# Attention and a depthwise convolution on one core: statistics of x closer together, conv weights prepared in image 2, matrices counted by the planner

## The chip, the core and the metric

The kernel runs on one core of a Trainium2 chip. A core has five engines that work side by side, each through its own list of instructions in order: TensorE (PE in the profile), VectorE (DVE), ScalarE (ACT), GpSimd (POOL) and SyncE (SP), which here only issues transfers. ACT and POOL issue transfers too. An instruction that waits on its engine holds up all that is queued behind it. The metric is the device time of one execution in microseconds (us).

## The reference

The input x has 16 images of 384 channels and 32 x 32 pixels, float32. Two layers with a residual follow each other:

```python
x = x + attention(gn(x))        # 8 heads of 48, 1024 tokens, q k v and a projection with bias
x = x + dwconv(gn(x), w_sym)    # 7 x 7 depthwise, padding 3
# gn(v): (v - mean) / sqrt(var + 1e-5) over each of 32 groups of 12 channels
# w_sym: mean of the weight and its three rotations by 90 degrees
```

In the text, "x" is the input and "x1" is the result of the first layer.

## The kernel before

The channels lie on the partitions, in three tiles of 128 per image. For each of the 16 images, PE makes q and k (`qk_step`, L417) and v (`v_step`, L443), then for 4 pairs of heads the scores (`s_step`, L468), whose exponential ACT takes (L476), and their product with v (`av_step`, L484), which also gives the sums for the softmax. These sums go through DRAM to a layout in which DVE inverts them (`invert`, L509) and back as a broadcast tile, with which DVE multiplies (`divide`, L520). Projection (`proj_step`, L537) and a transfer that adds x (L552) make x1. Its statistics come from ACT (`x1_means`, `x1_squares`), go through DRAM on POOL's queue to a layout by group, through DVE (`x1_aggregate`, L277) and ACT (`groups_x1`, L283 to 285) to a scale and a shift, and back through DRAM on POOL's queue (`spread`: gr_x at L254, sc_x at L258). ACT then normalises x1 (xn, L334). The depthwise convolution is 49 taps per channel tile on DVE (`conv_tap`, L602), each one a multiply and add of a shifted picture; three chains of taps, one per channel tile, run in turn. While PE does image b + 1, DVE does the taps of image b.

The last two images share the convolution with PE. There, for two of three channel tiles (one is split), matmuls with small diagonal matrices do it (`conv_on_pe`, L708). The matrices are made on DVE by `conv_matrices` (L666, four products each, two calls in the last image) from `wsh` and `eye`, which `conv_prepare` makes on POOL: a memset of `zero`, two transfers to DRAM, sixteen small ones back to `wsh`, eight that write zero borders in DRAM, and four small instructions for `eye`. In the kernel before it is called in image 1, after the first eight steps (L1214).

The scale of the input x is needed ahead of each image. Image 0 does its own at the start, image 1 by `x_channels` and `x_groups`, which use the Newton steps of `inverse_sigma` on DVE (L207 to L222). All the others are done in one stream during image 0: `stream_in` loads the 42 tiles (L350), `stream_stats` takes BN statistics (L357), `stream_gather` and `stream_groups` turn them by way of DRAM into `x_sc`. `stream_groups` ends with a power on POOL (L392).

The order of the instructions is written by a planner in the kernel's Python, which keeps two clocks: `clock` for PE and `vclock` for DVE. `after(wait, cost, f)` puts work in a heap with a due time and what it will take of DVE; `catch_up` lets DVE's list run up to PE's clock: due work first, otherwise the next tap, at the price of `us_tap`. A due time decides only a place in the lists, and every engine then runs its list as its waits allow. The prices that matter here are the 0.045 us that `us_tap` adds per tap in the last image (`late_us`) and the work of `conv_matrices`, which has no price.

At the end of the last image there is a different path (`divide_at_once`, L563 to L566, `proj_part`, L574, `residual`, L583): DVE inverts the sums directly (L565), PE projects, DVE adds and takes statistics, PE averages them by group (`groups_on_pe`, L302), and the taps and matmuls of what is left of images 14 and 15 follow, until `conv_on_pe_end` (L723) and the last output.

Of the kernel before, what the change touches and what calls it, by code (L numbers as in the profile page):

```python
# [44 lines left out]
def kernel(  # L45
# [64 lines left out]
    def run(general):  # L110
        tag = "g" if general else "f"
        with ExitStack() as stack:
# [233 lines left out]
            def stream_in(b, k):  # L346
                if not many:
                    many["bs"] = npool.tile([P, B - 2, NK, 12], F32, tag="xn1", name="bs_all")
                many[b, k] = rpool.tile([P, N], F32, tag="x1", name=f"xs_{b}_{k}")
                nc.gpsimd.dma_start(  # L350
                    many[b, k], x[b, k * P : (k + 1) * P].rearrange("p h w -> p (h w)")
                )

            def stream_stats(b, k):
                t = many.pop((b, k))
                for h in range(2):
                    nc.vector.bn_stats(  # L357
                        many["bs"][:, b - 2, k, 6 * h : 6 * h + 6], t[:, h * HALF : (h + 1) * HALF]
                    )
# [22 lines left out]
            def stream_groups():  # L382
                M = B - 2
                mv = small.tile([P, 4, 2], F32, tag="mva", name="mv_all")
                nc.vector.memset(mv, 1.0)
                for q in range(4):
                    n = min(P, M * GROUPS - q * P)
                    nc.vector.bn_aggr(mv[0:n, q], many["gs"][0:n, q])
                af = small.tile([P, 4, 2], F32, tag="afa", name="af_all")
                ve = small.tile([P, 4], F32, tag="vea", name="ve_all")  # L390
                nc.vector.tensor_scalar(ve, mv[:, :, 1], EPS, None, ALU.add)
                nc.gpsimd.tensor_tensor(af[:, :, 0], ve, mhalf, ALU.pow)  # L392
                nc.vector.scalar_tensor_tensor(
                    af[:, :, 1], mv[:, :, 0], -1.0, af[:, :, 0], ALU.mult, ALU.mult
                )
                gr_d = ddram.tile([M * GROUPS, PER, 2], F32, tag="gra", name="gr_all")
                with nc.allow_non_contiguous_dma(reason="once"):
                    for q in range(4):
                        n = min(P, M * GROUPS - q * P)
                        nc.gpsimd.dma_start(  # L400
                            gr_d[q * P : q * P + n],
                            af[0:n, q].unsqueeze(1).to_broadcast([n, PER, 2]),
                        )
                    rows = gr_d.rearrange("(b g) e s -> b (g e) s", b=M)
                    for k in range(NK):
                        nc.gpsimd.dma_start(
                            x_sc[:, 2:, k, :], rows[:, k * P : (k + 1) * P].rearrange("b p s -> p b s")
                        )
# [252 lines left out]

            def conv_matrices(n, dst):

                dst = dst[:, 0 : SH * 2 * KS * CH].rearrange("p (i t c) -> p i t c", i=SH, c=CH)
                for i in range(SH):
                    nc.vector.tensor_tensor(  # L666
                        dst[:, i],
                        eye.unsqueeze(1).to_broadcast([P, 2 * KS, CH]),
                        wsh[:, n, i].rearrange("p b d -> p (b d)").unsqueeze(2).to_broadcast(
                            [P, 2 * KS, CH]  # L670
                        ),
                        ALU.mult,
                    )
                mats[PE_K[n]] = dst

            def conv_store(b, k):
                nc.sync.dma_start(xds[b, k][:, PAD * W : (PAD + H) * W], xn1s[b, k])
# [138 lines left out]
            def after(wait, cost, f):  # L816

                nonlocal count
                count += 1
                heapq.heappush(later, (now() + wait, count, cost, f))  # L820

            def us_tap(dy, dx):
                late_us = 0.045 if clock > last_image else 0.0
                rows = H - abs(dy)
                if tuple(active[0][0:2]) == SHARED:
                    rows = min(H - max(0, dy), SPLIT) - max(0, -dy)
                return (rows * (W - abs(dx)) + (128 if len(active) > 1 else 268)) / 955 + late_us
# [239 lines left out]
            issue(chunks.popleft())  # L1067
            every = [(b, k) for b in range(2, B) for k in range(NK)]
            for n, bk in enumerate(every):
                after(3.0 * n, 0.0, lambda bk=bk: stream_in(*bk))  # L1070
                after(3.0 * n + 10.0, 1.4, lambda bk=bk: stream_stats(*bk))
            after(3.0 * len(every) + 14.0, 0.0, stream_gather)
            after(3.0 * len(every) + 34.0, 3.6, stream_groups)

            EARLY = NP * (B - 4)

# [92 lines left out]
            for b, n0, size in [  # L1169
                (b, b * PER_B + sum(SIZES[:g]), SIZES[g]) for b in range(B) for g in range(len(SIZES))  # L1170
            ]:
                r = n0 - b * PER_B
                if n0 == NS - PER_B:
                    last_image = clock
                if r % (2 * NT) == 0 and r // (2 * NT) < NK:
                    while chunks and chunks[0][1:] <= (b, r // (2 * NT)):
                        issue(chunks.popleft())
                for n in range(n0, n0 + size):
                    s_step(n)
                clock += (size * US_STEP + US_TURN) / 2  # L1180
                if r == 0:
                    for i in range(NT // 2):
                        issue(("v", b, i))
                ending = b == B - 1 and r + size == PER_B
                if ending:
                    catch_up(clock)
                    divide_at_once(NP * b + NP - 1, 0)
                    vclock += 4.2
                    for o in range(NK):
                        proj_part(b, o, (0, 1))  # L1190
                    loads(1)
                    clock += 2 * US_PROJ
                else:
                    catch_up(clock)
                    act_slot(4.5)
                    other(n0 + size, False)
                for n in range(n0, n0 + size):
                    av_step(n)
                    u, h, i = n // (2 * NT), n // NT % 2, n % NT
                    if i == NT - 1:  # L1200
                        take(u, h)
                clock += (size * US_STEP + US_TURN) / 2
                if n0 // (2 * NT) < (n0 + size) // (2 * NT):
                    finish((n0 + size) // (2 * NT) - 1)
                if ending:
                    catch_up(clock)
                    assert not invs and not waiting
                    fast_finish(b)
                else:
                    other(n0 + size, True)  # L1210
                if b == B - 4 and r == 32:
                    after(0.0, 2.0, check_early)
                if b == 1 and r == 0:
                    conv_prepare()  # L1214
                if b == B - 1:

                    if once("mat_0", r >= 16):
                        mat = flat2(xpool.tile([P, NK, N], F32, tag="x", name="mat_0"))
                        conv_matrices(0, mat)
                        late["w3"] = mat[:, 2 * SH * KS * CH :][:, 0:C]  # L1220
                    if once("w", r >= 32 and b - 1 in x1_stats):
                        nc.sync.dma_start(wp, w4[:, 0:NK])
                        nc.sync.dma_start(late["w3"], w4[:, NK])
                    if once("mat_1", r >= 24):
                        conv_matrices(1, flat2(qkpool.tile([P, 2, N], F32, tag="qk", name="mat_1")))
                    if once("ones", r >= 32):
                        t = opool.tile([P, N], F32, tag="o", name="masks_1")
                        nc.sync.dma_start(t, masks.rearrange("p b c -> p (b c)"))
                        late["masks"] = t.rearrange("p (b c) -> p b c", c=P)
                if b == B - 1:  # L1230
                    if r >= 32 and (b, 0) not in x1s and all(c[0] > b - 2 for c in active):
                        for k in range(NK):
                            x1s[b, k] = rpool.tile([P, N], F32, tag="x1", name=f"x1_{b}_{k}")
                            nc.gpsimd.dma_start(
                                x1s[b, k], x[b, k * P : (k + 1) * P].rearrange("p h w -> p (h w)")
                            )
                if b == B - 1 and r in (32, 40, 48):
                    loads(1)
# [63 lines left out]
```

## Time and profile before

| | |
|---|---|
| median of 4 runs | 2942.09 us (2939.54 to 2944.22) |
| the profiled execution | 2943.35 us |
| its span, first to last instruction | 2941.3 us |
| PE busy | 2903.3 us, 99% |
| DVE busy | 2573.6 us, 88% |
| ACT busy | 1442.6 us, 49% |
| POOL busy | 192.6 us, 7% |
| mean granted clock of PE | 0.994 |

The profile gives times in us from the start of the span. A line of a timeline has the start, the duration, the engine, the line of the kernel, the operation, what it writes and reads, and how many instructions were merged; in brackets stands how long the engine was idle before it, and what ended the wait. A line of waits has who waited, for whom, the total, how often, and the longest. A line of stretches has the stretch and its length, then busy time and count for PE, PE's weight loads, DVE, ACT and POOL, then PE's granted clock, the share of the DMA engines and GB/s.

### The profile page before, as it was taken

How to read it: one execution, taken by the hardware profiler on the slowest of the kernel's cores; microseconds unless marked ns; L12 is line 12 of the kernel's file. 1: busy time of each engine (PE TensorE's matmuls, PEld its weight loads, DVE VectorE, ACT ScalarE, POOL GpSimd, SP SyncE). 2: the span in 40 equal slices, each digit the busy share in tenths (PEclk: the TensorE clock that was granted, in tenths of full speed). 3: DMA queues.
4: the chain of work that ended last, by engine and by line, in shares of the span. 5: the costliest groups of instructions: out<-in, count | busy, mean ns of one | idle time of the engine just before them, and what ended most of it. 6: DMA issues, size and time to landing. Idle time of an engine off the chain costs nothing.

```text
span 2941.3 us, 30279 instructions
## 1 busy us (share of the span) xinstructions
PE 2903.3 (99%) x11554; PEld 1175.6 (40%) x11554; DVE 2573.6 (88%) x2546; ACT 1442.6 (49%) x1724; POOL 192.6 (7%) x305
## 2 busy tenths in 40 slices
PE   8999999999999999999999999999999999999987
PEld 4343343433434343343434434343343434334333
DVE  4322998989999898999989899898999989899898
ACT  2545545464454555445464554546545365554610
POOL 2113000000100001000000100000010000100000
PEclk9999999999999999999999999999999999999999
DMA  6423012120302203022220301213021221301424
GB/s 233 143 63 70 16 35 69 37 68 16 83 22 42 69 21 84 16 40 64 42 63 24 84 20 35 69 29 76 16 64 41 42 63 27 83 16 35 117 61 116
DMA packets 72539, 169.84 MB, mean 58 GB/s; under 512 B 30416, under 2 KB 32352, under 8 KB 70848
## 3 DMA queue, kind: packets, MB, share of 16 engines
q0 software_dynamic: 29456, 96.08, 12.9%
q1 hardware_dynamic: 41328, 68.44, 9.8%
q10 hardware_dynamic: 1600, 3.28, 0.5%
q8 instruction: 93, 1.52, 0.2%
q14 instruction: 62, 0.51, 0.1%
HBM read 119.92 MB, written 29.36 MB: 51 GB/s over the span
## 4 chain that ended last, share of the span: by engine, by line


## 5 line engine op out<-in xcount | busy, mean ns | idle before, releaser
L602 DVE SCALAR_TENSOR_TENSOR x<-xn,wsym,x 128x899 f32<-128x899 f32 (+11 forms) x2181 | 2372.2, 1169 | 109.2 <-ACT xn L334 109.2
L476 ACT ACTIVATE e<-ps_s 128x1024 f32<-128x1024 f32 x1024 | 952.5, 1054 | 55.7 <-PE ps_s L468 52.8
L468 PE MATMUL ps_s<-qk 48*128 48x512 f32 x4096 | 916.3, 597 | 3.0 <-ACT qk L424 3.0
L484 PE MATMUL acc<-e,v 128*64 128x512 f32 x4096 | 907.2, 595 | 0.0
L468 PEld LDWEIGHTS ps_s<-qk 48*128 48x128 f32 x4096 | 377.4, 186 | 538.1 <-ACT e L476 256.9
L484 PEld LDWEIGHTS acc<-e,v 128*64 128x64 f32 x4096 | 283.1, 137 | 608.1 <-issue 599.0
L417 PE MATMUL ps_qk<-x,wqk 128*128 128x512 f32 x1152 | 508.7, 598 | 2.4 <-DVE x L330 2.4
L495 ACT COPY o<-acc 128x512 f32<-128x512 f32 x128 | 75.1, 587 | 603.9 <-PE acc L484 603.8
L417 PEld LDWEIGHTS ps_qk<-x,wqk 128*128 128x128 f32 x1152 | 217.5, 191 | 289.9 <-issue 287.4
L443 PE MATMUL ps_v<-wv,x 128*128 128x384 f32 x768 | 252.0, 488 | 0.0
L537 PE MATMUL ps_proj<-o,wp 128*128 128x512 f32 x540 | 234.6, 593 | 1.0 <-DMA o<-o 1.0
L424 ACT COPY qk<-ps_qk 128x1024 f32<-128x1024 f32 x96 | 96.5, 1006 | 241.7 <-PE ps_qk L417 241.6
L443 PEld LDWEIGHTS ps_v<-wv,x 128*128 128x128 f32 x768 | 144.8, 190 | 109.5 <-ACT e L476 12.1
L520 DVE TENSOR_TENSOR o<-o,inv 128x1024 f32<-128x1024 f32 x63 | 77.3, 1227 | 99.9 <-DMA inv<-inv 80.2
L552 POOL DMA_DIRECT2D x<-in_x x45 | 39.2, 870 | 1869.3 <-ACT x L545 1736.3
L537 PEld LDWEIGHTS ps_proj<-o,wp 128*128 128x128 f32 x540 | 102.3, 190 | 128.3 <-issue 124.2
L452 ACT COPY v<-ps_v 128x384 f32<-128x384 f32 x128 | 55.1, 483 | 185.6 <-PE ps_v L443 185.6
L545 ACT ACTIVATE x<-ps_proj,bp 128x1024 f32<-128x1024 f32 x45 | 50.1, 1113 | 184.7 <-PE ps_proj L537 184.7
L334 ACT ACTIVATE xn<-x,sc_x 128x1024 f32<-128x1024 f32 x46 | 53.8, 1231 | 101.6 <-DMA sc_x<-gr_x 68.5
L509 DVE RECIPROCAL rec<-sums 128x16 f32<-128x16 f32 x63 | 16.0, 254 | 78.5 <-DMA sums<-sum 78.5
L708 PE MATMUL ps_conv<-sh,mat 128*32 128x464 f32 (+7 forms) x784 | 72.9, 527 | 1.6 <-DMA sh<-xd 1.6
L357 DVE BATCH_NORM_STATS2 bs_all<-xs 128x6 f32<-128x512 f32 x84 | 51.9, 680 | 12.1 <-DMA xs<-in_x 12.1
(113 smaller groups left out, 505.8 us busy)
## 6 DMA issues: line engine op xcount, KB each, us to landing
x<-in_x POOLq DMA_DIRECT2D x90, 512.0 KB, 5.6
inv<-inv SPq DMA_DIRECT2D x126, 256.0 KB
out<-x POOLq DMA_DIRECT2D x48, 512.0 KB, 7.5
xs<-in_x POOLq DMA_DIRECT2D x42, 512.0 KB, 6.1
qk<-qk SPq DMA_DIRECT2D x96, 128.0 KB
o<-o SPq DMA_DIRECT2D x90, 64.0 KB
sh<-xd SPq DMA_DIRECT2D x36, 160.0 KB
sh<-xd ACTq DMA_DIRECT2D x20, 160.0 KB
```

The lines of the kernel that those rows point to most:

```text
L417: nc.tensor.matmul(ps[:, h, :], lhsT=wqk[:, k, s, t, :], rhs=xns[b][:, k, h * HALF : (h + 1) * HALF], start=(k == 0), stop=(k == NK - 1),)
L424: nc.scalar.copy(halves(qks[u][:, s, :]), ps)
L443: nc.tensor.matmul(ps[:, j, 0:C], lhsT=xns[b][:, k, t * P : (t + 1) * P], rhs=wv[:, k, :], start=(k == 0), stop=(k == NK - 1),)
L452: nc.scalar.copy(dst.rearrange("p (h d) -> p h d", d=D + 1)[:, :, 0:D], ps[:, j, 0:C].rearrange("p (h d) -> p h d", d=D),)
L468: nc.tensor.matmul(ps[:, j, :], lhsT=qks[u][r, 1, i * P : (i + 1) * P], rhs=qks[u][r, 0, h * HALF : (h + 1) * HALF], start=True, stop=True,)
L476: nc.scalar.activation(es[n], ps, AF.Exp, scale=SCALE)
L484: nc.tensor.matmul(accs[u, h][64 * j : 64 * j + 64, :], lhsT=v_of(u, i, j), rhs=e[:, j, :], start=(i == 0), stop=(i == NT - 1),)
L495: nc.scalar.copy(os_[u][:, h * HALF : (h + 1) * HALF], accs.pop((u, h)))
L520: nc.vector.tensor_tensor(os_[u], os_[u], invs.pop(u), ALU.mult)
L537: nc.tensor.matmul(ps[:, h, :], lhsT=wp[:, t, o * P : (o + 1) * P], rhs=os_[NP * b + t][:, h * HALF : (h + 1) * HALF], start=(t == 0), sto ...
L602: nc.vector.scalar_tensor_tensor(acc, xn1s[b, k].rearrange("p (h w) -> p h w", w=W)[:, iy, ix], wsym[:, k, dy + PAD, dx + PAD : dx + PAD + 1],
L708: nc.tensor.matmul(pss[b, k][CH * i : CH * (i + 1), h, :].rearrange("p (y x) -> p y x", x=W)[:, y0:, ox], lhsT=mats[k][:, i, d0 * KS + dx ...
```

## The change

Five edits. `stream_groups` calls `inverse_sigma` on DVE for all groups in place of a power on POOL between two DVE instructions. The stream's tiles are planned 2.0 us apart instead of 3.0, with the gather and the groups moved accordingly, and their costs to the planner are 0.6 and 6.0 instead of 0.0 and 3.6. `conv_prepare` is called in image 2 after the step group that starts at 40, instead of image 1 after the first. `conv_matrices` advances `vclock` by 2.2 per call. `late_us` is 0.02 instead of 0.045.

```diff
                 af = small.tile([P, 4, 2], F32, tag="afa", name="af_all")
-                ve = small.tile([P, 4], F32, tag="vea", name="ve_all")
-                nc.vector.tensor_scalar(ve, mv[:, :, 1], EPS, None, ALU.add)
-                nc.gpsimd.tensor_tensor(af[:, :, 0], ve, mhalf, ALU.pow)
-                nc.vector.scalar_tensor_tensor(
-                    af[:, :, 1], mv[:, :, 0], -1.0, af[:, :, 0], ALU.mult, ALU.mult
-                )
+                inverse_sigma(af, mv[:, :, 0], mv[:, :, 1], "all")
...
             def conv_matrices(n, dst):
+                nonlocal vclock
...
                 mats[PE_K[n]] = dst
+                vclock += 2.2
...
-                late_us = 0.045 if clock > last_image else 0.0
+                late_us = 0.02 if clock > last_image else 0.0
...
-                after(3.0 * n, 0.0, lambda bk=bk: stream_in(*bk))
-                after(3.0 * n + 10.0, 1.4, lambda bk=bk: stream_stats(*bk))
-            after(3.0 * len(every) + 14.0, 0.0, stream_gather)
-            after(3.0 * len(every) + 34.0, 3.6, stream_groups)
+                after(2.0 * n, 0.0, lambda bk=bk: stream_in(*bk))
+                after(2.0 * n + 10.0, 1.4, lambda bk=bk: stream_stats(*bk))
+            after(2.0 * len(every) + 14.0, 0.6, stream_gather)
+            after(2.0 * len(every) + 34.0, 6.0, stream_groups)
...
-                if b == 1 and r == 0:
+                if b == 2 and r == 40:
                     conv_prepare()
```

## The prediction

> **What bounds the kernel.** I read the page first (the chain that ended last is empty there), then PE's waits, then the timelines around every PE gap, and the stretches at the end.
>
> ```profile
> PE 2903.3 (99%) x11554; PEld 1175.6 (40%) x11554; DVE 2573.6 (88%) x2546; ACT 1442.6 (49%) x1724; POOL 192.6 (7%) x305
> ```
>
> PE is idle for 38.0 of 2941.3 us: 8.1 before 20 us, 18.2 after it ends at about 2923, the rest in few places. The waits of PE name them:
>
> ```profile
> PE ps_proj L574 <- DVE o L566: 5.8, 1, 5.8
> ...
> PE ps_s L468 <- ACT qk L424: 3.0, 2, 1.9
> ...
> PE ps_conv L708 <- DMA sh<-xd: 1.6, 1, 1.6
> ```
>
> So only what removes a PE gap, or shortens the head or the tail, can pay. The 1.9 us is in image 1. The timelines of POOL, ACT and PE there:
>
> ```profile
> 259.24 0.29 ACT L285 ACTIVATE af_x<-mv_x,af_x 32x1 f32<-32x1 f32 x1
> ...
> 260.51 0.90 POOL L660 TENSOR_TENSOR eye<-eye,ident 128x32 f32<-128x32 f32 x3
> ...
> 261.71 0.64 POOL L254 DMA_DIRECT2D gr_x<-af_x  x1 [0.30 <-issue]
> ...
> 270.65 3.50 ACT L334 ACTIVATE xn<-x,sc_x 128x1024 f32<-128x1024 f32 x3 [8.39 <-DMA sc_x<-gr_x]
> ...
> 272.06 1.13 PE L468 MATMUL ps_s<-qk 48*128 48x512 f32 x4
> ...
> 275.10 7.97 PE L468 MATMUL ps_s<-qk 48*128 48x512 f32 x28 [1.91 <-ACT qk L424]
> ...
> 283.00 7.09 PE L484 MATMUL acc<-e,v 128*64 128x512 f32 x32
> ```
>
> The scale of image 0's x1 was ready at 259.53, but POOL was still in `conv_prepare` (244.29 to 261.4) and issued it at 261.71. ACT then waited 8.39 us, the qk evictions (L424) stood behind it, and PE stopped. The same place one image later, with no `conv_prepare` ahead:
>
> ```profile
> 445.83 3.50 ACT L334 ACTIVATE xn<-x,sc_x 128x1024 f32<-128x1024 f32 x3 [4.59 <-DMA sc_x<-gr_x]
> ...
> 451.04 7.14 PE L468 MATMUL ps_s<-qk 48*128 48x512 f32 x32
> 458.11 7.09 PE L484 MATMUL acc<-e,v 128*64 128x512 f32 x32
> ```
>
> From the first L468 to L484 it takes 7.07 us here, and 10.94 in image 1: 3.87 us are lost there. The stretches show why that is more than the wait of 1.91, and the same in the tail (the first figures are PE's busy time, the 0.50 is the granted clock):
>
> ```profile
> 276.00:278.00 2.00, 2.00 (x8) 0.99 (x8) 2.00 (x4) 1.79 (x2) 0.00 (x0) 0.50 0.97 383
> ...
> 2836.00:2839.00 3.00, 0.38 (x1) 0.38 (x2) 2.91 (x3) 0.00 (x0) 0.00 (x0) 0.50 0.00 0
> 2839.00:2841.00 2.00, 2.00 (x3) 0.79 (x3) 1.84 (x3) 0.00 (x0) 0.00 (x0) 0.50 0.00 0
> ```
>
> In the tail DVE is the bound: from 2747.66 it runs without a gap to 2840.6, and its last instruction closes the kernel, 5 us after PE's last matmul:
>
> ```profile
> 2834.43 3.36 DVE L565 RECIPROCAL inv<-ps_sum 128x512 f32<-128x512 f32 x1
> ...
> 2838.62 6.57 PE L574 MATMUL ps_proj<-o,mat 128*128 128x512 f32 x10 [5.78 <-DVE o L566]
> ...
> 2927.75 1.22 DVE L723 TENSOR_TENSOR x<-ps_conv,x 128x1024 f32<-128x1024 f32 x1
> ```
>
> **What the Trainium skill says.** "TensorE: Matmul & The Clock Gate", Part 1: PE's clock is halved after an idle window of about 3.4 us and restored after a busy one, and the windows run freely, so where they fall differs from run to run. The trace agrees, with less idle than that: half clock from 275.9 to 279.3, after a gap of 1.9 us, and from 2835.9 to 2842.7, stretches of 3.4 and 6.8 us. "DMA: Bandwidth & Descriptors", Anatomy of one DMA: a DMA from GpSimd costs about 2 us fixed. The hop gr_x to sc_x here takes 4.3 us from issue to issue, and wsh 1.9 to landing. The same page, Issuing engines are not separate DMA queues: all share 16 engines; it fits sum to sums taking 3.5 us beside `conv_prepare` (262.29 to 265.77) against 2.2 one image later.
>
> **The change, part by part.** In the instruction orders of the changed program PE, ACT and SP are unchanged; only DVE and POOL differ.
>
> *conv_prepare in image 2.* 17.1 us of POOL work leave the place ahead of gr_x. gr_x is then issued 0.3 us after 259.53, at 259.8; by the row at 445.83 xn begins 5.29 us after the qk matmuls (440.54), so at 261.56 + 5.29 = 266.9 instead of 270.65. Three applies take 3.5, to 270.4; the first qk is ready at 266.9 and the second at 272.1, as in image 2. PE does not stop: gain 3.87 us in this profile, made of 2.16 waiting and half of 3.41 = 1.71 at half clock. Even if sc_x comes only 1.9 us earlier (what POOL gives back), xn starts at 268.8 and about 3.4 of it remains. But the clock part needs the idle 1.91 to fall well inside one window, (3.41-1.91)/3.41 = 44% of positions, so in a median I count half of 1.71: 2.16 + 0.85 = 3.0. From there to image 14 all is paced by PE, and DVE waits for xn every image (109 us in 15 waits), so the shift is kept.
> At its new place it stands behind the loads of x for image 3 (issued by 453.0), and POOL has nothing else until 575.55, a wait of 122.56 us. Its first memset needs a tile whose last reader is a divide; even with the one at 504.98 it is done by 523. The x1 adds (L552) are behind it, 52 us later; the inverse that reuses its tile is loaded at 559. Cost 0; with the cover gone, up to 17.1 us.
>
> *x statistics at 2.0 instead of 3.0.* 42 loads and 84 BN statistics of 0.68 us come earlier. DVE did them in image 0 in gaps (it idles 46.5 us at the first reciprocal), so they cost nothing. What moves is image 1's own scale: x_channels and x_groups now stand behind more of them, and the reciprocal of pair 1 behind these. bs_x follows the divide at 111.43 and one more statistic: it ends at 117.5 (116.2 before). gs_x is then issued at 120.2; nine statistics lie ahead of the aggregate, five loaded, four whose loads are issued behind gs_x and land from about 126 to 130 (6.1 us each, 1.25 apart). Aggregate 131, 2.3 for the Newton steps, gr_x 134, sc_x issued at 138.3 and landed at 140.8. ACT takes it at 147.69 after eight exponentials, so 7 us are spare, and 2.2 more ahead of the next copy. Cost 0; bounds 0 to what exceeds 149.7. The group aggregates then end near 158, when the third reciprocal (158.47) gets its sums; projection needs the last divide at 209.84.
>
> *Newton instead of the power on POOL.* 12 more DVE instructions at 0.18 us pitch = 2.2 us, less a POOL hop of 1.3 (172.93 to 174.26). DVE idles 29 us right behind, and image 2 needs x_sc at 284. Cost 0.
>
> *The last image's order.* Matrices are now counted (2 x 2.2 us) and taps 0.025 us cheaper. As built: both reciprocals and divides of the last pairs come two or three taps earlier, and L565/L566 twice: two taps (812 and 841 elements, 2.1 us) that stood ahead now stand behind. L566 ends at 2836.5 instead of 2838.56, so PE's gap falls from 5.78 to 3.7 us. But DVE gets the same instructions: what follows begins 2.1 us earlier and has 2.1 us more to do. As many taps stand ahead of the wait at L1101 as before. So the end moves by nothing, except for DVE's own waits on PE (2.72 at L316, 0.3 at L583): PE at half clock for 2.8 instead of 4.1 us saves up to 0.65 there. I take 0.4, between 0 and 2.9. The sums of pairs 61 and 62 were requested at 2760.3 and 2790.7, more than 10 us ahead of their moved reciprocals: no new wait.
>
> **Sum.** Against the profiled execution: 2941.3 - 3.87 - 0.4 = 2937.0, plus 2.05 around the span = 2939.1. That execution (2943.35) lies 1.26 above the median of the runs, which a clock window that not all runs pay would explain. On the median: 2942.09 - 3.0 - 0.4 = 2938.7.
>
> **Rivals.**
> 1. *The tail passes its gain on.* For: PE's gap shrinks by 2.1 and DVE waits 7.4 us for PE and POOL after 2840. Against: those waits move as a whole. It would be 2942.09 - 3.0 - 2.9 = 2936.2.
> 2. *The transfer is late anyway.* For: sc_x took 4.6 us from issue to apply at 266, beside six qk copies on SP; if these, and not POOL, hold it, the change does not do what it says. Against: 2.4 us at 2721.79. Gain 0.2: 2941.9.
> 3. *Slower: image 1's scale late in image 0.* Behind more statistics and loads, sc_x misses 149.7, the last moment at which three applies of 3.56 meet the qk matmuls at 153.29. Each microsecond more is paid in full, and 1.7 for the clock. It eats the gain of 3.4 from a landing at about 151.4; at 160 the kernel is at 2942.1 - 3.4 + 10.3 + 1.7 = 2950.7. Against: 9 us between 140.8 and 149.7.
>
> **How the numbers follow.** This kernel's runs tell a difference from about 0.2% (5.9 us). Forecast 0.66 (own range 2936.5 to 2940.5), rival 1 0.15, rival 2 0.10, rival 3 0.09. Faster by over 0.2% means below 2936.2: half of rival 1 (0.075) and a seventh of the forecast, for where the clock windows fall (0.095), 0.17. Slower, above 2948: rival 3, 0.09. Same: the rest, 0.74. The range for 8 in 10 reaches from rival 1's lower half to just over no gain: 2935.0 to 2943.0.
>
> **What would show it.** Right: no PE wait on ACT qk in image 1, gr_x issued near 259.8, and L468 to L484 in 7.1 us; ACT's apply near 147.7 without a wait; `conv_prepare` in POOL's hole of image 2; PE's gap at L574 near 3.7 us; DVE still last. Wrong: a new wait at L334 in image 0, xn still near 270, or a PE gap in image 2 or 3.

## The result, and the profile after

| | before | after |
|---|---|---|
| median | 2941.31 us, 60 runs (2937.76 to 2946.55) | 2937.64 us, 40 runs (2935.0 to 2940.11) |
| ratio after to before | | 0.9987, 95% interval 0.9982 to 0.9991 |
| span of the profiled execution | 2941.3 us | 2935.2 us |

The change takes about 3.7 us away, 0.13% of the time. The forecast was 2938.7 from 2942.09, a ratio of 0.9988. In a later set of runs (e11 below) the same two kernels lie 6.9 us apart, so the size of the gain is less certain than one interval says. The two profiled executions differ by more than the medians (their last DVE instructions by 5.84 us), so not all that separates these two traces is worth an explanation.

The lines are numbered anew: L597 is the tap, L463 the scores, L479 their product with v, L419 the copy of q and k, L569 the late projection, L561 the late divide. First the page after, its engine line:

```profile
PE 2901.0 (99%) x11554; PEld 1172.0 (40%) x11554; DVE 2575.4 (88%) x2558; ACT 1441.5 (49%) x1724; POOL 204.6 (7%) x304
```

DVE has 12 instructions more, the Newton steps; POOL one fewer, the power. PE has 2.3 us less although its matmuls are the same. PE's waits after:

```profile
PE ps_proj L569 <- DVE o L561: 2.5, 1, 2.5
...
PE ps_s L463 <- ACT qk L419: 1.7, 2, 1.1
PE ps_conv L705 <- DMA sh<-xd: 1.6, 1, 1.6
```

The gap in the tail fell from 5.8 to 2.5. The waits for ACT's qk fell from 3.0 to 1.7, not to 1.1: a stall of 0.6 is left in image 1. The timelines after, in image 0 and then in image 1:

```profile
134.82 0.61 POOL L254 DMA_DIRECT2D gr_x<-af_x  x1 [10.57 <-DVE x_mean L362]
139.03 0.77 POOL L258 DMA_DIRECT2D sc_x<-gr_x  x1 [3.61 <-DMA gr_x<-af_x]
...
147.61 3.55 ACT L334 ACTIVATE x<-x,sc_x 128x1024 f32<-128x1024 f32 x3
...
259.93 0.60 POOL L254 DMA_DIRECT2D gr_x<-af_x  x1 [15.56 <-ACT af_x L285]
...
264.21 2.41 SPq L428 DMA_DIRECT2D qk<-qk  x4
...
264.28 0.78 POOL L258 DMA_DIRECT2D sc_x<-gr_x  x1 [3.75 <-issue]
...
269.24 3.50 ACT L334 ACTIVATE xn<-x,sc_x 128x1024 f32<-128x1024 f32 x3 [7.06 <-DMA sc_x<-gr_x]
...
273.69 6.62 PE L463 MATMUL ps_s<-qk 48*128 48x512 f32 x28 [0.59 <-ACT qk L419]
...
280.24 7.09 PE L479 MATMUL acc<-e,v 128*64 128x512 f32 x32
```

In image 0 the scale of image 1's x is there in time: ACT's row at 147.61 has no wait. In image 1 POOL now stands idle until af_x is written and issues gr_x at 259.93, 1.8 us earlier than before. But sc_x lands only 5.0 us after its issue, so xn begins at 269.24 (270.65 before) and PE stops for 0.59 us where it stopped for 1.91. With the clock whole, the way from the first L463 (271.98) to L479 takes 8.26 us; it was 10.94 before.

### The profile page after: what moved, and what is told of

Read it like the earlier page. It is cut to its first block, busy times and chain, and to the rows that moved or that the text cites. A ratio compares the mean times of both kernels' runs of the same rounds, so it can differ in the third digit from the quotient of the medians.

```text
span 2935.2 us, 30293 instructions
## 1 busy us (share of the span) xinstructions
PE 2901.0 (99%) x11554; PEld 1172.0 (40%) x11554; DVE 2575.4 (88%) x2558; ACT 1441.5 (49%) x1724; POOL 204.6 (7%) x304
## 5 line engine op out<-in xcount | busy, mean ns | idle before, releaser
L597 DVE SCALAR_TENSOR_TENSOR x<-xn,wsym,x 128x899 f32<-128x899 f32 (+11 forms) x2181 | 2372.5, 1171 | 111.7 <-ACT xn L334 111.7
L463 PE MATMUL ps_s<-qk 48*128 48x512 f32 x4096 | 915.1, 596 | 1.7 <-ACT qk L419 1.7
L479 PE MATMUL acc<-e,v 128*64 128x512 f32 x4096 | 907.2, 595 | 0.0
L463 PEld LDWEIGHTS ps_s<-qk 48*128 48x128 f32 x4096 | 375.9, 185 | 537.1 <-ACT e L471 259.7
L479 PEld LDWEIGHTS acc<-e,v 128*64 128x64 f32 x4096 | 283.0, 137 | 608.2 <-issue 599.3
L419 ACT COPY qk<-ps_qk 128x1024 f32<-128x1024 f32 x96 | 96.4, 1006 | 239.8 <-PE ps_qk L412 239.6
L705 PE MATMUL ps_conv<-sh,mat 128*32 128x480 f32 (+7 forms) x784 | 73.0, 527 | 1.6 <-DMA sh<-xd 1.6
L265 ACT ACTIVATE sq_x<-x,x_bs 128x1024 f32<-128x1024 f32 x45 | 51.2, 1140 | 16.9 <-DVE x_bs L947 16.9
```

The costliest lines, as they stand in the source:

```text
L419: nc.scalar.copy(halves(qks[u][:, s, :]), ps)
L463: nc.tensor.matmul(ps[:, j, :], lhsT=qks[u][r, 1, i * P : (i + 1) * P], rhs=qks[u][r, 0, h * HALF : (h + 1) * HALF], start=True, stop=True,)
L479: nc.tensor.matmul(accs[u, h][64 * j : 64 * j + 64, :], lhsT=v_of(u, i, j), rhs=e[:, j, :], start=(i == 0), stop=(i == NT - 1),)
L597: nc.vector.scalar_tensor_tensor(acc, xn1s[b, k].rearrange("p (h w) -> p h w", w=W)[:, iy, ix], wsym[:, k, dy + PAD, dx + PAD : dx + PAD + 1],
L705: nc.tensor.matmul(pss[b, k][CH * i : CH * (i + 1), h, :].rearrange("p (y x) -> p y x", x=W)[:, y0:, ox], lhsT=mats[k][:, i, d0 * KS + dx ...
```

## The experiments

Every run is compared with the kernel before, on the same chip. The runs came in three sets: e1 to e4, e5 to e8, and e9 to e12. Each set shared one chip; the last two sets have the same chip on record, and the kernel before took 2944.44 and 2944.6 us in them.

| run | median us | ratio to before | 95% interval | PE's stall in image 1 | L463 to L479 there | gap at L569 in the tail |
|---|---|---|---|---|---|---|
| before | | | | 1.91 | 10.94 | 5.8 |
| after | 2937.64 | 0.9987 | 0.9982 to 0.9991 | 0.59 | 8.26 | 2.5 |
| e1 prepare alone | 2942.15 | 0.9991 | 0.9982 to 0.9999 | 0 | 7.07 | 5.6 |
| e2 without prepare | 2943.8 | 0.9994 | 0.9986 to 1.0002 | 1.12 | 8.79 | 4.0 |
| e3 tail alone | 2944.74 | 0.9997 | 0.9989 to 1.0005 | 2.32 | 12.95 | 3.2 |
| e4 POOL busy | 2942.15 | 0.9992 | 0.9985 to 0.9998 | 2.31 | 9.99 | 3.8 |
| e5 scale late | 2943.36 | 0.9994 | 0.9985 to 1.0002 | 0 | 7.07 | 4.0 |
| e6 two taps behind | 2936.88 | 0.9973 | 0.9963 to 0.9984 | 0 | 7.76 | 1.3 |
| e7 divide later | 2932.96 | 0.9958 | 0.9945 to 0.9971 | 0 | 7.07 | 0 |
| e8 all filled | 2933.04 | 0.9958 | 0.9945 to 0.9970 | 0 | 7.31 | 0 |
| e9 prepare at step 24 | 2939.9 | 0.9985 | 0.9979 to 0.9992 | 0 | 7.07 | 5.5 |
| e10 waits filled | 2928.58 | 0.9945 | 0.9931 to 0.9959 | 0.77 | 8.44 | 0 |
| e11 after, beside | 2937.68 | 0.9976 | 0.9967 to 0.9985 | 0 | 7.07 | 3.8 |
| e12 copies later | 2940.88 | 0.9986 | 0.9980 to 0.9993 | 0 | 7.07 | 3.5 |

The stall is the wait of L463 for ACT's qk in image 1 that the profile lists, without the 1.1 us that every run has at the start. The kernel after has two ratios, 0.9987 in its own comparison and 0.9976 on the chip of the last two sets. Their intervals only just overlap, although its medians are alike (2937.64 and 2937.68): it is the kernel before that took 2941.31 us in one comparison and 2944.6 in the other. So much can a ratio differ from set to set, and a difference of 0.1% between runs on different chips means nothing. The medians do not say which part of the change brings what: in the first set e1, without the stall, and e4, with it, both took 2942.15 us. For that the traces carry the argument.

### The parts of the change alone

**e1**, the kernel before with only the call of `conv_prepare` moved:

```diff
-                if b == 1 and r == 0:
+                if b == 2 and r == 40:
                     conv_prepare()
```

> The kernel before with one edit: conv_prepare in image 2 after the step group at 40. My theory: nearly the whole gain of the change, 2.2 to 3.9 us less than before (ratio 0.9987 to 0.9993), the scale of image 0's x1 issued near 259.8 instead of 261.7, the wait of ACT at its first xn shorter by 1 to 4 us, and the stretch from the first L468 to L484 of image 1 at 8.3 us or less instead of 10.9. Rival, that the statistics or the tail make the gain: no difference (0.9997 to 1.0003).

The timelines of ACT and PE in e1, image 1 (there L468 and L484 are the scores and the product with v):

```profile
268.25 3.50 ACT L334 ACTIVATE xn<-x,sc_x 128x1024 f32<-128x1024 f32 x3 [4.35 <-DMA sc_x<-gr_x]
...
273.69 7.14 PE L468 MATMUL ps_s<-qk 48*128 48x512 f32 x32
```

All 32 score matmuls are one group without a wait, as in image 2, and L484 follows 7.07 us after. The move alone does to image 1 what the prediction said. In the median it brings 2.8 us, with an interval from 0.3 to 5.3.

**e2**, the kernel after with the call put back to image 1:

> The changed kernel with conv_prepare put back into image 1. My theory: the statistics, the Newton steps and the tail order together give 0 to 0.7 us, ratio 0.9997 to 1.0, and the PE wait on ACT qk in image 1 is back at 1.5 to 2 us. Rival, that these parts make the gain: 3 us and more, ratio 0.999 or less.

The stall comes back, but with 1.12 us, less than the 1.5 to 2 that were expected, and at full clock. The median stays 1.1 us below that of before, and the interval has 1 in it: what the rest of the change brings can't be told from nothing.

**e3**, the kernel before with only the planner's two prices changed:

```diff
+                nonlocal vclock
...
+                vclock += 2.2
...
-                late_us = 0.045 if clock > last_image else 0.0
+                late_us = 0.02 if clock > last_image else 0.0
```

> The kernel before with the two planner prices of the last image alone (2.2 per call of conv_matrices, 0.02 per tap). My theory: PE's gap at L574 falls from 5.8 to 3.7 us or less, and the end moves by 0 to 0.7 us, because DVE closes the kernel and has the same work; ratio 0.9997 to 1.0. Rival, that the tail passes on what PE gains: 2.1 to 2.9 us, ratio 0.9990 to 0.9993.

The gap in the tail falls to 3.2 us and the ratio is 0.9997, which can't be told from 1 either. PE's gain of 2.5 us in the tail is not seen in the median; but the interval reaches down to 3.2 us, so that rival 1, which gives the tail 2.9, is not ruled out by the median. The traces say more. From DVE's divide of pair 60 to its last addition the three traces with the old order (before, e1, e9) take 180.1 to 180.8 us, 180.6 in the mean; the seven with the new order and nothing else changed in the tail (after, e2, e3, e4, e5, e11, e12) take 179.4 to 180.1, 179.8 in the mean. The new order brings the end about 0.8 us, not 2.9. e6 and e7 below ask the tail more sharply.

### Is it POOL's time that delays the scale, or its place?

**e4**, the kernel after with 19 memsets of 128x1024 on POOL where the call stood before. They need about the same time of POOL, 19.1 us, but move nothing by DMA:

```diff
+                if b == 1 and r == 0:
+                    idle = tpool.tile([P, N], F32, tag="t", name="idle")
+                    for _ in range(19):
+                        nc.gpsimd.memset(idle, 0.0)
```

> The changed kernel with 19 memsets of 128 x 1024 on POOL (about 17 us, no transfers) where conv_prepare stood in image 1; the results of the kernel are the same. It tells POOL being busy from the transfers of conv_prepare. If POOL's time alone is the cause, the scale is issued near 261.5 again and the gain is lost but for 0.7 us: ratio 0.9997 to 1.0. If the transfers of conv_prepare slowed the scale on its way, the time stays near the changed kernel's, ratio 0.9987 to 0.9991, although the scale is issued late.

POOL's timeline in e4, and PE's:

```profile
243.15 19.14 POOL L1213 MEMSET idle<- 128x1024 f32 x19
262.23 0.61 POOL L254 DMA_DIRECT2D gr_x<-af_x  x1
...
274.04 6.62 PE L463 MATMUL ps_s<-qk 48*128 48x512 f32 x28 [2.31 <-ACT qk L419]
```

The last memset ends and gr_x follows in the same moment; ACT then waits 8.79 us for the scale (8.39 before) and PE stops for 2.31. Memsets reproduce the stall, so it is POOL's queue that made the scale late, and not `conv_prepare`'s transfers. The median does not decide it: 0.9992 lies nearer to what was expected if the transfers were to blame (0.9987 to 0.9991) than to 0.9997 to 1.0, and the interval reaches from the one to the other. In this trace the section still took 0.95 us less than before, because the clock stayed whole; why the median shows no more of the loss is open.

**e9**, the kernel before with the call at step 24 of image 1, behind gr_x and sc_x:

```diff
-                if b == 1 and r == 0:
+                if b == 1 and r == 24:
                     conv_prepare()
```

> The kernel before with conv_prepare called at step 24 of image 1 and not at step 0, so that its 17 us of POOL stand behind gr_x, sc_x and the loads of the next x, but still in image 1. Theory (its place ahead of gr_x is what costs, image 2 is not needed): gr_x is issued as soon as af_x is there (within 1 us), PE's stall at L468 in image 1 is under 0.6 us and L468 to L484 takes 7.1 to 8.3 us (10.94 before); ratio 0.9990 to 0.9993, as with the call in image 2 (0.9991). Rival (POOL's 17 us are paid wherever they stand in image 1, by the loads of x for the residual that queue behind them): the stall comes back at another line in image 1 or 2, ratio 0.9998 or more.

gr_x is issued at 260.98 when af_x is written, there is no stall, and L468 to L484 takes 7.07 us. The ratio is 0.9985, no worse than with the call in image 2. So what counts is that the 17 us no longer stand ahead of gr_x; 24 steps later in the same image are as good as one image later in this section. In the medians the kernel after (e11, same set) is still 2.2 us faster than e9, so here the rest of the change brought something that e2 and e3 do not show. 1.1 us of it are in the tail: from the divide of pair 60 to the last addition e9 takes 180.82 us and e11 179.76.

### Why the scale still came late

**e12**, the kernel after with the six copies of left-over rows in image 1 issued with the last chunk first. SP then waits for that chunk, and the copies start at 272.36 instead of 264.21:

```diff
-                for t in range(NK):
+                for t in (2, 0, 1) if b == 1 else range(NK):
                     for j in range(2):
```

> The kernel after with the six copies of the left-over rows of image 1 (qk<-qk, 128 KB each on SP) issued in another order, the two for the last chunk first: SP waits for that chunk at about 273 us, so none of the six runs while sc_x of image 1 is under way. In the runs so far sc_x landed 4.6 to 5.0 us after its issue where the first copy was issued less than 0.2 us behind it or up to 2.2 us ahead (before, after, the tail alone), and 2.5 to 3.3 us where the copies came 0.34 us or more behind it, or had been issued 4 us ahead. Theory (the copies make sc_x late): sc_x lands 2.4 to 3.3 us after its issue, ACT applies at 266.7 to 267.6 (269.24 in the kernel after), the stall of 0.59 us at L463 is gone and L463 to L479 takes 7.07 us (8.26): 1.2 us, too little for the medians (0.9983 against 0.9987). Rival (the latency is chance or the transfer's own): 4 to 5 us as before, L463 to L479 at 8 us or more.

ACT's and PE's timelines in e12:

```profile
265.77 3.50 ACT L334 ACTIVATE xn<-x,sc_x 128x1024 f32<-128x1024 f32 x3 [4.35 <-DMA sc_x<-gr_x]
...
271.22 7.14 PE L463 MATMUL ps_s<-qk 48*128 48x512 f32 x32
278.28 7.09 PE L479 MATMUL acc<-e,v 128*64 128x512 f32 x32
```

sc_x was issued at 263.48, so it took 2.3 us to the apply, and the stall is gone. The other runs say the same; time from the issue of sc_x to the apply of xn, against the moment of the first copy (128 KB each, four in a row):

| first copy issued, after sc_x | run: us from issue to apply |
|---|---|
| 2.15 us ahead, to 0.02 us behind | e3 4.65, after 4.96, e10 4.90, e7 3.73 |
| 0.16 to 0.21 us behind | e6 4.41, before 4.61, e8 3.96, e11 3.72 |
| 0.34 to 0.42 us behind | e2 3.32, e1 2.46, e9 3.19, e5 3.12 |
| 4.0 us ahead, or not near | e4 2.79, e12 2.29 |

In image 1 a transfer of 3 KB that is issued with the copies, or while they run, takes 3.7 to 5.0 us; one that is issued a third of a microsecond ahead of them, or well apart from them, 2.3 to 3.3. In images 2 to 14 of the same traces the two groups overlap. Where the first copy came less than 0.25 us behind sc_x, it took 3.3 to 4.3 us (9 cases); where it came 0.27 to 1.3 us behind, 2.3 to 4.0, with a median of 2.8 (173 cases). So the order of the two issues makes a long time likely, but it does not fix it.

The median of e12 shows nothing of the 1.2 us. It is 3.2 us above that of the kernel after in the same set (e11), so the later copies are no improvement: in e12's trace PE lost 2.4 us again in a wait for the transfer o<-o in a projection of image 1. That wait lies between 0 and 4.0 us in the runs; whether the later copies had a part in it is open.

**e11**, the kernel after once more, beside e9, e10 and e12:

> The kernel after itself, as the yardstick beside the other runs of this set: ratio to the kernel before 0.9987 (0.9982 to 0.9991 in its own comparison). In its trace sc_x of image 1 lands 4 to 5 us after its issue if the first qk copy is again issued within 0.2 us of it, and 2.5 to 3.3 if not.

The copy came 0.21 us behind sc_x, and 3.72 us passed to the apply: between the two cases that were expected. xn began at 268.06 and PE did not stop. So a landing of 3.7 us is early enough. Of the runs with this order on POOL, a stall is listed only where the landing nears 5 us, as in the profiled execution of the kernel after and in e10. With 4.41 us in e6 and 3.96 in e8 no wait is listed, though the section took 7.76 and 7.31 us there; in e5, e7 and e11 it took 7.07.

### Rival 3: when is the scale of image 1 too late?

**e5**, the kernel after with 24 memsets on POOL ahead of gr_x of image 1, in image 0:

```diff
             def x_groups(b, st):
+                idle = rpool.tile([P, N], F32, tag="x1", name="idle")
+                for _ in range(24):
+                    nc.gpsimd.memset(idle, 0.0)
                 st.groups()
```

> The kernel after, with 24 memsets of 128x1024 on POOL put ahead of gr_x of image 1, whose tile nothing reads (in image 0; they lengthen only POOL's queue, at about 1.0 us each). It doubles the cost that rival 3 priced: image 1's scale late. In the kernel after gr_x was issued at 134.8 us and ACT applied the scale at 147.6 without a wait. Theory (the slack runs out at 149.7 us): POOL is through with the memsets at 148 to 149, gr_x follows at once, sc_x is issued 4.2 later and lands 2.5 to 5 after that, at 155 to 158; ACT waits 7 to 10 us at L334 in image 0 and PE stalls 5 to 8 us behind it, with a half-clock window or two (up to 3.4 us more). Time against the kernel before: 1.001 to 1.003. Rival (the exponentials behind the waiting ACT are hidden by what PE still has queued): PE stalls under 2 us, ratio 0.999.

POOL's, ACT's and PE's timelines in e5:

```profile
148.10 0.61 POOL L254 DMA_DIRECT2D gr_x<-af_x  x1
...
154.83 3.50 ACT L334 ACTIVATE x<-x,sc_x 128x1024 f32<-128x1024 f32 x3 [7.69 <-issue]
...
156.12 13.33 PE L412 MATMUL ps_qk<-x,wqk 128*128 128x512 f32 x24 [3.50 <-ACT x L334]
```

The mechanism is real: with gr_x 13.3 us later ACT waits, PE stops for 3.50 us, and the 24 matmuls take 13.33 us instead of 10.57 because the clock is halved behind the gap (the granted clock was 0.50 from 155 to 161). 6.3 us are lost, and 1.2 of them come back in image 1, where the profiled execution of the kernel after has its stall and this one none. But the latest moment is not 149.7: PE waited from 152.62 to 156.12, and started 1.29 us after the first apply began. PE needs one of the three applies to begin, so ACT could have begun at about 151 without a stall; this is an estimate from these times. The kernel after began at 147.61. The ratio of 0.9994 lies below the 1.001 to 1.003 that was expected. Against the kernel after on the same chip (e11) the median is 5.7 us higher, as is the span of the trace against that of the kernel after.

### What sets the end of the tail

**e6**, the kernel after with the two taps ahead of the last divide taken out there, so that they come later:

```diff
                 proj_part(b, 0, (NP - 2,))
-                tap(), tap()
                 divide_at_once(NP * b + NP - 1, 1)
```

> The kernel after with the two taps ahead of the last divide of the last image (first tap pair in fast_finish) taken out there, so that they come later on DVE: L560 and L561 run 2.1 us earlier and PE's wait for o at L569 (2.54 us) falls to about 0.4. Theory (DVE ends the kernel, its number of taps is the same): PE's part of the tail ends 2.1 us earlier, DVE's end moves only by what its own waits behind PE shrink (2.95 us at L316, so 0 to 2.1) : 0 to 2.1 us, about 1 by the profile. Rival 1 (what PE gains in the tail passes straight to the end): 2.1 us and the half clock of 3.4 us behind the gap as well, 3.8 in all. Ratio against the kernel before: theory 0.9985, rival 0.9975.

PE's wait and DVE's last addition, first in the kernel after and then in e6:

```profile
2831.08 6.26 PE L569 MATMUL ps_proj<-o,mat 128*128 128x512 f32 x10 [2.54 <-DVE o L561]
...
2921.91 1.22 DVE L720 TENSOR_TENSOR x<-ps_conv,x 128x1024 f32<-128x1024 f32 x1
```

```profile
2831.68 4.56 PE L569 MATMUL ps_proj<-o,mat 128*128 128x512 f32 x10 [1.29 <-DVE o L561]
...
2922.96 1.22 DVE L720 TENSOR_TENSOR x<-ps_conv,x 128x1024 f32<-128x1024 f32 x1
```

PE's gap falls to 1.29 us, not to the 0.4 that was expected, and the halved clock behind it is gone (ten matmuls in 4.56 us instead of 6.26). Counted from the last L463 group (2797.81 here, 2795.96 after), PE reaches its convolution 2.96 us earlier, but DVE's last addition comes only 0.80 us earlier (at 2922.96 against 2921.91). That is the theory's 0 to 2.1, about 1, in the trace. The ratio of 0.9973 taken alone agrees with rival 1's number (0.9975). But on this chip the kernel after (e11) has 0.9976, and the medians, 2936.88 and 2937.68, are 0.8 us apart, not the 3.8 of rival 1.

**e7**, the kernel after with one divide on DVE planned later. In the last image DVE stood for 5.39 us in front of the divide of pair 60, whose inverted sums were still on their way (6.57 us before). Here is that row, in DVE's timeline after:

```profile
2742.10 1.23 DVE L515 TENSOR_TENSOR o<-o,inv 128x1024 f32<-128x1024 f32 x1 [5.39 <-DMA inv<-inv]
```

The edit gives this divide, and no other, a later due time:

```diff
-                after(5.5 if u % NP == NP - 1 else 9.5, 1.3, lambda: finish3(u))
+                after(16.0 if u == U - NP else 5.5 if u % NP == NP - 1 else 9.5, 1.3, lambda: finish3(u))
```

> The kernel after with the divide of pair 60 (L515, where DVE waits 5.39 us for inv in the last image) planned later, behind five taps and the first four products for the conv matrices, which are 7 us of DVE work that waits for nothing. PE's order is as it was. Theory (DVE's own queue sets the end of the tail, PE has 5.7 us to spare there: its last matmul ends at 2915.0 and the last addition on DVE can start then): DVE's end comes 5 us earlier, ratio to the kernel before about 0.9970 (against 0.9987 for the kernel after). Rival (PE or the transfer sets the tail): same as the kernel after, 0.9987.

DVE's timeline in e7:

```profile
2727.15 14.68 DVE L597 SCALAR_TENSOR_TENSOR x<-xn,wsym,x 128x725 f32<-128x725 f32 x15
2741.75 2.23 DVE L662 TENSOR_TENSOR mat<-eye,wsh 128x448 f32<-128x448 f32 x4
2743.89 1.22 DVE L515 TENSOR_TENSOR o<-o,inv 128x1024 f32<-128x1024 f32 x1
...
2917.71 1.22 DVE L720 TENSOR_TENSOR x<-ps_conv,x 128x1024 f32<-128x1024 f32 x1
```

The divide has no wait any more; five taps and four products that stood behind it stand ahead of it. The last addition comes at 2917.71 instead of 2921.91, with PE's last scores at 2796.03 and 2795.96. So 4.3 of the 5.39 us reach the end; DVE is early enough at its two late reciprocals to wait 1.08 and 1.32 us there for PE. PE's gap at L569 is gone too. In the same set it is 3.9 us faster than e6, and 4.7 us faster than the kernel after on the same chip (e11), where 5 were expected. The ratio to the kernel before is lower than the expected 0.9970, which lies just inside its interval, as that of e11 is lower than 0.9987. DVE's queue from this divide on sets the end of the kernel, as the prediction had it.

**e8**, e7 and e6 together, with DVE's reading of a small sum that PE makes near the end (`ps_again`, L1098) behind the taps of one more conv piece:

> The two edits before together (no taps ahead of the last divide; the divide of pair 60 later), and DVE's reading of the check's sum (L1098, 1.87 us of wait) moved behind the taps of one conv piece. DVE loses 5.4 + 1.9 + 0 to 2.1 us of waits, PE 2.1 us and perhaps its half clock (1.7). Theory: DVE alone would end 7 to 9 us earlier, at 2913 to 2915 in the profiled execution of the kernel after, PE's last matmul at 2912.9 or earlier with 1.2 us of addition behind it: both meet, 7 to 8 us earlier, ratio to the kernel before 0.9960 to 0.9963. Rival (tail bound by PE or by transfers all along): 0.998 or above.

The ratio is a little below the theory's 0.9960 to 0.9963, and it did not come about in the way that was expected: there is no gain over e7 (0.9958 both), and the last addition is at 2917.75. PE's last matmul does not bound it, since PE ends at 2910.4. In e7 PE's gap was gone already, so taking taps away ahead of the divide only let DVE arrive earlier at the reciprocal L560, whose sums PE makes at 2823: DVE's wait there rose from 1.32 to 3.36 us, which uses up the 1.89 that L1098 had given. A filler helps only where work is ahead of the wait, and e6's edit takes work from there.

**e10**, e7 with that reading later, and one more tap in front of two other waits for PE, at L316 and L321:

```diff
                     on_pe()
                     between()
+                    between()
...
                     average(NK, d)
                     between()
+                    between()
```

> The kernel with the divide of pair 60 later, and three of DVE's remaining waits in the tail filled: one more tap ahead of L316 (1.28 us of wait), one more ahead of L321 (1.67) and the reading of the check's sum (L1098, 1.89) behind the taps of one conv piece. PE's order is the same. Theory (DVE bounds the tail until PE's last matmul plus one addition, at about 2912.0 in that profile, 5.7 us ahead of DVE's last instruction): 1.06 + 1.1 + 1.89 = 4.0 us less, ratio to the kernel before about 0.9945 (0.9958 without the fills). Rival (the waits come back at the next release from PE or POOL): 1 us or less, 0.9955 or more.

The waits in DVE's timeline in e10, where they are L317 and L323:

```profile
2841.71 0.16 DVE L317 TENSOR_TENSOR d_x<-mn_x,ps_st_x 128x3 f32<-128x3 f32 x1 [0.25 <-PE ps_st_x L302]
...
2844.97 0.16 DVE L323 TENSOR_SCALAR d_x<-ps_st_x 128x3 f32<-128x3 f32 x1 [0.64 <-PE ps_st_x L302]
...
2914.66 1.22 DVE L722 TENSOR_TENSOR x<-ps_conv,x 128x1024 f32<-128x1024 f32 x1
```

1.28 and 1.67 us of wait have become 0.25 and 0.64, the 1.89 is gone, and PE does what it did. From the start of PE's convolution to the last addition it is 4.05 us less than in e7 (2834.04 to 2914.66 against 2833.04 to 2917.71). The ratio is the expected 0.9945, and beside the kernel after on the same chip 2928.58 to 2937.68, 9.1 us less. This version is the fastest of all that ran.

## Why the prediction was right, step by step

**conv_prepare in image 2: right in its mechanism and in its sum, with one term too small.** gr_x was to be issued at 259.8 and was at 259.93. xn was to begin at 266.9 and began at 269.24; L463 to L479 was to take 7.07 us and took 8.26. The term that was mis-sized is the time of sc_x. xn at 266.9, which I took from image 2's row, leaves it 2.8 us from its issue to the apply (259.8, and 4.3 to the issue); in image 2 it had taken 2.3, and here 4.96 were measured. It meets the copies on SP, as e12 and the table in its section show. The prediction gave these copies no time in the new program, and they moved along with sc_x: they stand in SP's queue right behind `sums`, and the hop from `sum` to `sums` took 1.56 us instead of 3.48 (1.54 in e4, with memsets in place of `conv_prepare`'s transfers), so the first copy was issued at 264.21 instead of 266.22. Rival 2 was right in that these copies can hold the transfer, but wrong in that the change then brings nothing: POOL gives its 1.8 us back in any case. With `conv_prepare` or the memsets ahead of gr_x the section took 10.94, 12.95, 8.79 and 9.99 us, 3.6 more than 7.07 in the mean. With them elsewhere it took 8.26, 8.44, 7.76, 7.31 and six times 7.07, 0.35 more. The gain by these traces is 3.2 us; the prediction had 3.0. The medians agree with that (2.8 us in e1, 4.7 in e9), but e4 shows that they do not prove it. `conv_prepare` now stands behind the loads of the next x in image 2, from 465.45 on, and no PE wait came with it there.

**The halved clock: right to be counted by half.** After the stalls of 1.91 and 2.32 us (before, e3) the granted clock fell to 0.50, for 3.4 and 6.8 us; after those of 1.12 and 2.31 (e2, e4) it did not fall. The stretches of e3 behind its stall (the last three figures are the granted clock, the share of the DMA engines and GB/s):

```profile
282.00:285.00 3.00, 3.00 (x10) 1.24 (x8) 3.00 (x5) 2.05 (x2) 0.00 (x0) 0.50 0.69 212
```

And those of e4, behind a stall as long:

```profile
277.00:281.00 4.00, 4.00 (x19) 1.20 (x18) 4.00 (x5) 4.00 (x5) 0.00 (x0) 1.00 0.23 49
```

The prediction supposed that the idle time has to fall inside one window of 3.41 us, and the traces bear this out. Within each of the 14 traces the changes of the granted clock lie whole multiples of 3.413 us apart; in the trace of before, 275.88 and 2835.87 are 750 of them apart. With these steps as the windows, the 1.91 us of before lie in one window, and so do 2.15 of e3's 2.32. In e4 an edge at 272.92 cuts the 2.31 us into 1.19 and 1.13, and in e12 one at 390.17 cuts a wait of 2.39 into 0.99 and 1.40; there the clock stayed whole. Between 60 us and the last matmuls, all 14 windows at full clock with 1.91 us or more of idle PE were followed by the halved clock, and none with 1.79 or less was. This agrees with what the Trainium skill, "TensorE: Matmul & The Clock Gate", Part 1, says of windows that run freely; but an idle time much below its window was enough.

**x statistics at 2.0: right.** Aggregate 131, gr_x 134, sc_x issued at 138.3, ACT at 147.69: measured 131.35, 134.82, 139.03 and 147.61, without a wait. Rival 3's mechanism exists (e5); its limit was mis-sized, 149.7 instead of about 151, since it asked for three applies where one is enough to begin.

**Newton on DVE: nothing showed against a cost of 0.** It was not tried alone. The kernel after pays its 12 instructions, and nothing waits for them in its trace.

**The last image's order: right in the trace.** PE's gap was to fall from 5.78 to 3.7 us. In the seven traces with the new order that are named at e3 it was 2.5 to 4.0, 3.5 in the mean; with the old one 5.5 to 5.8. The end was to move by 0.4; between DVE's divide of pair 60 (2747.66 before, 2742.10 after) and its last addition (2927.75 and 2921.91), 0.28 us were gained, and 0.8 in the mean of those traces. Rival 1 had no more than that: e6 gives PE 3 us and the end 0.8, e7 gives DVE 5.4 us and the end 4.3. (DVE's waits after 2840, which the prediction puts at 7.4 us there, add up to 7.6.)

**The sum: close, in part by luck.** 3.4 us were forecast and 3.7 measured, but 6.9 on the chip of the last two sets, where the kernel before is slower and the kernel after is not. The traces give 3.2 us for image 1 and 0.8 for the tail, 4.0 together. What the rest of the 6.9 is stays open.

**What the two profiles differ by besides.** Of the 5.84 us between them, 2.76 are there at L479 of image 1, 0.28 in the tail, and 1.2 in DVE's wait for pair 60, which was 6.38 us in the kernel after once more (e11). The other 1.6 come in small steps in images 4 to 12, in part at projections, where PE waits for transfers by a few tenths in one run and not in the other. This is not the change's doing by any evidence here, and the medians don't have it.

## What to carry to other kernels

Before a block of setup work is put on an engine that also issues transfers, look for the next transfer that is issued from the same queue and ask who waits for it: in these traces 17 us behind it cost nothing, ahead of it they cost over 3 us on another engine. A small transfer's time should be taken from a row with the same neighbours on the queues, not from the same line in a quieter image. And where two engines both have gaps in a tail, as here, fill those of the engine whose last instruction closes the kernel, and give it work that stands ahead of the wait; shortening the other engine's gap moves the end by little.

## What was not expected of the hardware

- A 3 KB transfer took 3.7 to 5.0 us in image 1 where four copies of 128 KB were issued about with it, and 2.3 to 3.3 where they came 0.34 us or more behind it. In later images the same order showed only as a tendency.
- A gap of 2.31 us left PE's clock whole in one run, and one of 1.91 halved it in another. What told them apart was how much of the gap lay in one window of 3.41 us: 1.91 and more halved the clock, 1.79 and less never did.
- PE's waits for the transfer o<-o at the projections lay between 0 and 4.0 us at the longest in executions of nearly the same program. They make a difference of 1 or 2 us in one pair of traces worthless without the rows that it comes from.
